# A six-stage transformer kernel: cross attention in pairs of steps on TensorE, two ternary weights quantized in an earlier stage, and another ending

## The chip, the cores and the metric

The kernel runs on one core of a Trainium2 chip. A core has five engines with an instruction queue each: TensorE (PE; its weight loads are listed as PEld), VectorE (DVE), ScalarE (ACT), GpSimd (POOL) and SyncE (SP), which issues most of the DMAs. The metric is the device time of one execution in microseconds (us); the time before is the median of three runs.

## The reference

All of it is float32. `x` is (4, 512, 512); `ctx_2048` is the context. Two layers of three stages each, and a layer norm after each stage:

```python
x = _layernorm(x + _L0_attn_ref(x, q_w, q_b, kv_w, kv_b, o_w))    # A: self-attention with rotary embedding
x = _layernorm(x + _L0_xattn_ref(x, ctx, ctx, gamma))             # B: cross attention over features
x = _layernorm(x + _L0_ffn_ref(x, w_gate, w_up, w_down))          # C: ternary feed-forward
x = _layernorm(x + _L1_attn_ref(x, ...))                          # D
x = _layernorm(x + _L1_xattn_ref(x, ctx, mask))                   # E
x = _layernorm(x + _L1_ffn_ref(x, ...))                           # F: 4-bit feed-forward, RMS norm of its output
```

The stages that the change touches, cut to what matters:

```python
def _L0_xattn_ref(q, k, v, gamma):       # 8 heads of 64 features
    qk = einsum('bhdq,bhdl->bhql', qh, kh) / sqrt(64)
    return gamma * einsum('bhql,bhdl->bhdq', softmax(qk), vh)

def weight_quant(w):                     # _L0_ffn_ref: each of gate, up and down becomes -1, 0 or 1, times a scale
    scale = 1.0 / clip(mean(abs(w)), 1e-5)
    return clip(round(w * scale), -1.0, 1.0) / scale

def _L1_ffn_ref(x, ...):                 # its last lines
    y = einsum('bsi,hi->bsh', h, w_down)
    return y / sqrt(mean(y * y, axis=-1) + 1e-6)
```

The rounding needs the mean of a whole weight first, so each weight is read twice.

## The kernel before

**Order of the work.** The four batches of the six stages make 24 tasks, A0 to F3, in the order of `ORDER`: A0 A1 A2 A3 B0 and so on. Each task is a Python generator that emits instructions and yields. `lanes` (L1234 on) takes a piece from each of at most two live tasks in turn; the next task starts when the newest has said "next" and its own batch has left the stage before. Besides, `BESIDE` names background generators, which are advanced by one piece in each round while given tasks run: "C0" (`l0_ffn_scales`) from A1 to A3, "C" (`l0_ffn_weights`) from B0 to B2. `Pipe.later(n, f)` puts a piece of work off by n ticks of its generator. The recorded program then goes through a scheduler, which keeps data dependences and may pull an instruction forward on its engine; `issue_after(ins)` puts what is emitted behind an instruction of the same engine. Each engine works off its queue in order.

**Memory.** PSUM has eight banks under one tag; `pa` and `pb` take a bank (512 float32 a partition). In SBUF, tiles of 2 KB a partition come from rings: `o` (69), `t` (13), `x` (12) and `w` (4).

**Stage A** (`l0_attn`, L330 on). In each batch TensorE makes q and k in eight tiles (`qk`), ScalarE moves each out with its bias (L340, tile `z`), `turn` does the rotary embedding (DVE L349 times sine, POOL L352 times cosine), `join` adds on POOL (L357), and `split` makes a high part on ScalarE (L143, `qkh`) and a low part on DVE (L146, `qkl`), so that three matmuls (L154 to L156) stand for one in float32. POOL also adds `bvo` to `x` (L408) and makes the low parts of the next batch's input (`xTl`, L146). Then come values `v`, scores `as`, softmax, transposes `ap` and `pv`.

**Stage B** (`l0_xattn`, L457 on). A task has 16 steps: four pairs of heads (n) times four row tiles (i). In one step TensorE makes the scores of two heads with three split products each (L526, six matmuls on 64 rows, tile `bs`). One tick later `soft` takes the maximum on DVE (L474) and the exponential on ScalarE (L476, tile `be`), and `norm` takes the reciprocal on DVE (L480) and multiplies on POOL (L482). Six ticks later `turn` transposes (L248, eight transposes of 128x128, tile `bT`) and copies each result to SBUF (L489, `bpT`; three of four on ScalarE, one on DVE). One more tick later `out` multiplies with the context (L498, 64 columns wide, tile `bo`, accumulated over the four row tiles). After the fourth, `add` (L503) and the layer norm's statistics follow on DVE. In each step one yield ends the piece, and the context of the next batch is loaded beside (`l0_xattn_ctx`, `kf`, `kh`, `kl`).

**Ternary weights.** Gate (`wg_t`), up (`wu_t`) and down (`wd_t`) have 16 chunks of 128x512 each. In A1 to A3, `l0_ffn_scales` loads each chunk into a `w` buffer and sums its absolute values on DVE (L558), and makes mean and scale (L566 to L572). In B0 to B2, `l0_ffn_weights` loads each of the 48 chunks again and quantizes it: two DVE instructions (L587: times the scale plus a large number, which rounds; L588: clip), and a cast to bf16 on ScalarE (L596) into a `tb` tile, two chunks a tile, which stays until stage C's matmuls have read it.

**The end** (`l1_ffn`, b = 3). After the last matmul of F3 (L1168, tile `facc`) ScalarE squares the four results with row sums (L1214), DVE makes the reciprocal root with integer tricks and three Newton steps (`rsqrt`, L166 to L176), adds to `x` (L1220), takes the layer norm's statistics (L211, L212), makes a second root of the same kind and normalizes four tiles (L235); SyncE stores them (L238).

Of the kernel before, what the change touches and what calls it, by code (L numbers as in the profile page):

```python
# [22 lines left out]
P = 128  # L23
NT = 4
# [44 lines left out]
class Net:  # L69
    def __init__(self, ctx, tc, args):  # L70
# [22 lines left out]
        self.gu_codes = scratch("gu_codes", (22, P, 512))  # L93
        self.xd = [args["x"]] + [scratch(f"x{i}", (B, S, D)) for i in range(1, 6)] + [args["out"]]
# [235 lines left out]
    def l0_attn(self, b):  # L330
# [7 lines left out]
        def evac(ps, w, m):  # L338
            z = zs[w, m] = self.t("z")
            nc.scalar.activation(z, ps, AF.Identity, bias=self.qkb[:, w * NT + m : w * NT + m + 1], scale=1.0 if w else P ** -0.5)  # L340
            if m % 2:
                pipe.later(1, turn, w, zs[w, m - 1], z)
# [114 lines left out]
    def l0_xattn(self, b):  # L457
# [26 lines left out]
        def turn(n, es, j, po):  # L484
            pTs = []
            for h in range(2):
                pt = self.transpose4(es[h], j, "bT")
                pT = self.t("bpT")
                (nc.scalar.copy if h == 0 or j % 2 else nc.vector.tensor_copy)(pT, pt)  # L489
                pTs.append(pT)  # L490
            pipe.later(1, out, n, j, po, pTs)

        def out(n, j, po, pTs):
            if j == 0:
                po.append(self.pb("bo"))
            for h in range(2):
                c = n * P + h * 64
                nc.tensor.matmul(po[0][h * 64 : h * 64 + 64, :], cT[j][:, c : c + 64], pTs[h], start=j == 0, stop=j == NT - 1)  # L498
            if j == NT - 1:
                pipe.later(1, add, n, po[0])  # L500
# [8 lines left out]
        yield  # L509
        for n in range(NT):  # L510
            u, es, po = us.pop(n), [[], []], []
            for i in range(NT):
                pipe.tick()
                if (n, i) == (0, 2) and b + 1 < B:
                    self.bg["B", b + 1] = self.l0_xattn_ctx(b + 1)
                if b + 1 < B and ("B", b + 1) in self.bg:
                    next(self.bg["B", b + 1], None)
                if i == 0 and n + 2 < NT:
                    scaled(n + 2)
                sm = self.s("bsm", 6, 8)  # L520
                ps = [self.pa("bs") for h in range(2)]

                for m, (l, r) in enumerate(((0, 0), (1, 0), (0, 1))):
                    for h in range(2):
                        q = slice(h * 64, h * 64 + 64)
                        nc.tensor.matmul(ps[h], u[l][q, i * P : (i + 1) * P], k[n][r][q, :], start=m == 0, stop=m == 2)  # L526
                for h in range(2):
                    pipe.later(1, soft, ps[h], sm, h, i, es)
                pipe.later(1, norm, sm, es, i)
                pipe.later(6, turn, n, es, i, po)  # L530
                yield "next" if 4 * n + i == B_NEXT else None
# [11 lines left out]
    def l0_ffn_scales(self):  # L543

        nc = self.nc
        self.had = self.c("had", [P, P], F32R)
        self.had16 = self.load(self.c("had16", [P, P]), self.a["had16"])
        f = self.t("had")
        nc.gpsimd.dma_start(f[:, 0:P], self.a["had"])
        pipe = Pipe()  # L550
        pipe.later(3, nc.vector.tensor_copy, self.had, f[:, 0:P])
        for name in self.TERNARY:
            chunks = self.ternary_chunks(name)
            part = self.c(name + "_abs", [P, len(chunks)])

            def absum(f, n):
                with self.tc.issue_after(self.mark.ins):
                    nc.vector.tensor_reduce(part[:, n : n + 1], f, AX.X, ALU.add, apply_absolute_value=True)  # L558

            for n, (k, c, ap) in enumerate(chunks):  # L560
                pipe.tick()
                pipe.later(1, absum, self.load(self.w("tw"), ap), n)
                yield
            yield from pipe.drain()
            m = self.c(name + "_mean", [P, 4])
            nc.vector.tensor_reduce(m[:, 2:3], part, AX.X, ALU.add)  # L566
            yield
            ps = self.pb("tot")
            nc.tensor.matmul(ps[:, 0:1], self.ones, m[:, 2:3], start=True, stop=True)
            yield  # L570
            nc.vector.tensor_scalar(m[:, 0:1], ps[:, 0:1], 1.0 / (len(chunks) * P * 512), 1e-5, ALU.mult, ALU.max)
            nc.vector.reciprocal(m[:, 1:2], m[:, 0:1])  # L572
            self.mean[name], self.scale[name] = m[:, 0:1], m[:, 1:2]

    def l0_ffn_weights(self):

        nc = self.nc
        yield from self.bg["C0"]
        pipe = Pipe()
        order = [("wg_t", x) for x in self.ternary_chunks("wg_t")]  # L580
        up = [("wu_t", x) for x in self.ternary_chunks("wu_t")]
        order = [e for c in range(4) for e in order[4 * c : 4 * c + 4] + up[4 * c : 4 * c + 4]]
        order += [("wd_t", x) for x in self.ternary_chunks("wd_t")]
        cur = []

        def quant(name, k, c, f):
            nc.vector.tensor_scalar(f, f, self.scale[name], MAGIC, ALU.mult, ALU.add)  # L587
            nc.vector.tensor_scalar(f, f, MAGIC + 1.0, MAGIC - 1.0, ALU.min, ALU.max)  # L588
            pipe.later(1, put, name, k, c, f)

        def put(name, k, c, f):
            if not cur:
                cur.append(self.o("tb", BF16, 1024))
            o = cur[0][:, 0:512] if len(cur) == 1 else cur[0][:, 512:1024]
            cur.append(o)
            nc.scalar.activation(o, f, AF.Copy, bias=-MAGIC)  # L596
            self.tern[name][k, c] = o
            if len(cur) == 3:
                cur.clear()

        for name, (k, c, ap) in order:
            pipe.tick()
            pipe.later(1, quant, name, k, c, self.load(self.w("tw"), ap))
# [512 lines left out]
    def l1_ffn(self, b):  # L1116
# [31 lines left out]
        def gate(o):  # L1148
            nc.scalar.activation(o, o, AF.Silu)
# [44 lines left out]
        if b + 1 < B:  # L1194
# [16 lines left out]
            return  # L1211
        for i in range(NT):
            sq = self.t("fsq")
            nc.scalar.activation(sq, acc[i], AF.Square, accum_out=ss[:, i : i + 1])  # L1214
            if i % 2:
                yield
        nc.vector.tensor_scalar(ve, ss, 1.0 / 512.0, 1e-6, ALU.mult, ALU.add)
        r = self.rsqrt(ve, fm[:, 8:20])
        for i in range(NT):
            nc.vector.scalar_tensor_tensor(x[i], acc[i], r[:, i : i + 1], x[i], ALU.mult, ALU.add)  # L1220
            self.ln_stats(x[i], i, ln)
            if i % 2:
                yield
        self.finish(pipe, x, ln, 5, b)
        yield from pipe.drain()
# [35 lines left out]
def body(tc, args, phases=range(6)):  # L1261
    with ExitStack() as ctx:
# [4 lines left out]
        net.bg = {("B", 0): net.l0_xattn_ctx(0), "C0": net.l0_ffn_scales(), "C": net.l0_ffn_weights(), "D": net.l1_attn_weights(), "F0": net.l1_ffn_codes(), "F": net.l1_ffn_weights()}  # L1267
# [82 lines left out]
```

## Time and profile before

| what | value |
|---|---|
| median of three runs | 1586.2 us (1585.69 to 1587.84) |
| profiled execution | 1587.75 us |
| its span, first to last instruction | 1586.0 us |
| mean granted clock of TensorE | 0.993 |
| PE busy | 1515.5 us (96%), 8222 matmuls |
| DVE busy | 1239.8 us (78%) |
| ACT busy | 1014.6 us (64%) |
| POOL busy | 666.0 us (42%) |
| DMA | 192.31 MB, mean 121 GB/s |

All durations below come from the profiled execution; its own time is 1.75 us over its span. An instruction's row in a timeline gives its start in us from the span's start, its duration, its engine and line, what it writes and reads, and in brackets the engine's idle time before it and what ended that. A group's row gives the number of instructions, the busy time in us, the mean of one in ns, and the idle time before them. "Slices" are 40 equal parts of the span with the busy share in tenths. A busy TensorE is not TensorE at its peak, since its matmuls overlap and their ends are modelled; the distances between their starts tell more.

### The profile page before, as it was taken

The numbers are of one execution on the slowest core, as the hardware profiler recorded it, in microseconds if no ns is written. First come the engines' busy times: TensorE is split into PE (matmuls) and PEld (weight loads), VectorE is DVE, ScalarE is ACT, GpSimd is POOL, SyncE is SP. The second block draws the span as 40 slices with busy tenths as digits, with TensorE's granted clock in tenths as the row PEclk, the third lists the DMA queues.
The fourth block names the chain that finished last, engine by engine and source line by source line (L and its number), as shares of the span: only waits on it lengthen the run. The fifth ranks groups of instructions, "written<-read, shape, count | busy, mean of one in ns | idle before, by whom it ended". The sixth has DMA issues, their size and how long they took to land.

```text
span 1586.0 us, 25593 instructions
## 1 busy us (share of the span) xinstructions
PE 1515.5 (96%) x8222; PEld 1092.0 (69%) x8222; DVE 1239.8 (78%) x2676; ACT 1014.6 (64%) x2193; POOL 666.0 (42%) x672
## 2 busy tenths in 40 slices
PE   8999999999999999899999999999999999999995
PEld 6888785444544664477777768777687767787874
DVE  6486589999976688778577697766886897889896
ACT  5333337888878877787696765968635455545552
POOL 6663663555535303430435323353234344434341
PEclk9999999999999999999999999999999999999998
DMA  7053344455114644653444435543426630020101
GB/s 254 29 166 114 121 155 136 141 173 184 62 57 123 220 150 131 204 178 116 134 109 122 111 131 153 156 112 91 136 99 219 236 107 30 1 80 1 54 1 53
DMA packets 134149, 192.31 MB, mean 121 GB/s; under 512 B 17264, under 2 KB 52080, under 8 KB 134016
## 3 DMA queue, kind: packets, MB, share of 16 engines
q1 hardware_dynamic: 129888, 182.23, 36.3%
q0 software_dynamic: 4128, 8.46, 2.1%
q8 instruction: 65, 1.06, 0.3%
q14 instruction: 68, 0.56, 0.1%
HBM read 117.75 MB, written 47.71 MB: 104 GB/s over the span
## 4 chain that ended last, share of the span: by engine, by line
PE 61%; DVE 17%; ACT 8%; issue 7%; DMA 3%; POOL 3%; SPq 0%; DVEq 0%; ACTq 0%; POOLq 0%
PE fg L1185 7%; PE facc L1168 6%; PE dT L933 3%; DVE fg L1141 3%; DVE bsm L474 3%; PE pg L687 2%; PE pu L689 2%; PE dn L741 2%; ACT de L923 2%; PE had L755 2%; PE bo L498 2%; PE do L953 2%; PE qk L156 2%; PE qk L155 2%; PE qk L154 2%
## 5 line engine op out<-in xcount | busy, mean ns | idle before, releaser
L1141 DVE SCALAR_TENSOR_TENSOR fg<-fg,gs,fg 128x512 f32<-128x512 f32 x220 | 162.7, 744 | 29.1 <-ACT fg L1133 16.0
L923 ACT ACTIVATE de<-de,dm 128x128 f32<-128x128 f32 (+3 forms) x256 | 143.0, 563 | 11.4 <-DVE dm L919 11.0
L1185 PE MATMUL fg<-fxh,gu 128*128 128x512 f32 x352 | 140.4, 399 | 6.0 <-DVE fg L1141 4.3
L919 DVE CUSTOM_DVE_ANT_0 de<-ds,negm,thr 128x128 f32<-128x128 f32 (+3 forms) x256 | 126.3, 545 | 19.0 <-PE ds L908 15.8
L482 POOL TENSOR_SCALAR be<-be,bsm 128x512 f32<-128x512 f32 x128 | 96.4, 766 | 103.8 <-DVE bsm L480 68.2
L1185 PE MATMUL fg<-fxl,gu 128*128 128x512 f32 x352 | 137.3, 390 | 0.0
L664 POOL TENSOR_TENSOR hl<-g,hh 128x512 fp32r<-128x512 f32 x64 | 83.3, 1308 | 110.6 <-ACT hh L663 89.8
L1145 POOL TENSOR_TENSOR fg<-fg,fg 128x512 f32<-128x512 f32 x44 | 60.4, 1374 | 150.0 <-DVE fg L1141 54.7
L476 ACT ACTIVATE be<-bs,bsm 128x512 f32<-128x512 f32 x128 | 87.4, 690 | 31.1 <-DVE bsm L474 29.3
L845 POOL TENSOR_TENSOR dql<-dqf,dqh 128x512 fp32r<-128x512 f32 x32 | 41.4, 1294 | 150.6 <-ACT dqh L844 141.6
L933 PE MATMUL dT<-ident,de 128*128 128x128 f32 x640 | 91.3, 278 | 8.5 <-ACT de L923 6.4
L933 PEld LDWEIGHTS dT<-ident,de 128*128 128x128 f32 x640 | 71.7, 141 | 27.6 <-ACT de L923 14.8
L1185 PEld LDWEIGHTS fg<-fxh,gu 128*128 128x128 f32 x352 | 66.0, 188 | 31.2 <-DVE fg L1141 15.6
L474 DVE TENSOR_REDUCE bsm<-bs 128x1 f32<-128x512 f32 x128 | 83.3, 671 | 0.0
L498 PE MATMUL bo<-bpT,cT 128*64 128x512 f32 x256 | 77.0, 618 | 2.7 <-DVE bpT L489 1.4
L248 PEld LDWEIGHTS bT<-ident,be 128*128 128x128 f32 x512 | 54.9, 141 | 34.1 <-issue 10.4
L248 PE MATMUL bT<-ident,be 128*128 128x128 f32 x512 | 73.2, 281 | 3.7 <-POOL be L482 2.2
L1185 PEld LDWEIGHTS fg<-fxl,gu 128*128 128x128 f32 x352 | 66.1, 188 | 12.2
L352 POOL TENSOR_TENSOR z<-z,rope_cos 128x512 f32<-128x512 f32 x32 | 46.8, 1473 | 64.8 <-DVE zs L349 57.8
L1137 ACT ACTIVATE fg<-fg,gs 128x512 f32<-128x512 f32 x44 | 30.3, 689 | 67.3 <-PE fg L1185 67.2
L687 PE MATMUL pg<-qT,tb 128*128 128x512 bf16 x256 | 66.8, 381 | 4.5 <-ACT qT L649 2.8
L1133 ACT ACTIVATE fg<-fg,gs 128x512 f32<-128x512 f32 x88 | 60.1, 683 | 16.4 <-PE fg L1185 16.3
(342 smaller groups left out, 4673.2 us busy)
## 6 DMA issues: line engine op xcount, KB each, us to landing
x<-x SPq DMA_DIRECT2D x176, 256.0 KB, 3.0
had_scratch<-hw SPq DMA_DIRECT2D x64, 256.0 KB, 2.3
z<-had_scratch SPq DMA_DIRECT2D x64, 256.0 KB, 6.0
stk<-dqh SPq DMA_DIRECT2D x192, 64.0 KB, 2.1
tw<-in_wg_t SPq DMA_DIRECT2D x32, 256.0 KB, 3.8
tw<-in_wu_t SPq DMA_DIRECT2D x32, 256.0 KB, 3.7
tw<-in_wd_t SPq DMA_DIRECT2D x32, 256.0 KB, 2.8
p<-in_gu_p SPq DMA_DIRECT2D x22, 256.0 KB, 3.1
```

The costliest lines, as they stand in the source:

```text
L248: self.nc.tensor.transpose(pt[:, i * P : (i + 1) * P], srcs[i][:, j * P : (j + 1) * P], self.ident)
L474: nc.vector.tensor_reduce(sm[:, h : h + 1], ps, AX.X, ALU.max, negate=True)
L476: nc.scalar.activation(e, ps, AF.Exp, bias=sm[:, h : h + 1], accum_out=sm[:, 2 + h : 3 + h])
L482: nc.gpsimd.tensor_scalar(es[h][i], es[h][i], sm[:, 4 + h : 5 + h], 1.0, ALU.mult, ALU.mult)
L498: nc.tensor.matmul(po[0][h * 64 : h * 64 + 64, :], cT[j][:, c : c + 64], pTs[h], start=j == 0, stop=j == NT - 1)
L687: nc.tensor.matmul(pg, tern["wg_t"][k, c][:, m], qT[k], start=k == 0, stop=k == NT - 1)
L919: nc.vector.tensor_tensor_reduce(es[i], ps, self.negm[:, 384 - P * i :], -1.0, self.thr[:, i : i + 1], ALU.add, ALU.min, n4[:, i : i + 1])
L923: nc.scalar.activation(es[i], es[i], AF.Exp, bias=n4[:, i : i + 1], scale=-1.0, accum_out=den[:, hh * 4 + i : hh * 4 + i + 1])
L933: nc.tensor.transpose(pt[:, o + (i - j) * P : o + (i - j + 1) * P], es[i][:, j * P : (j + 1) * P], self.ident)
L1141: self.emitted["DVE"] = nc.vector.scalar_tensor_tensor(y[u], ps, s, y[u], ALU.mult, ALU.add)
L1168: nc.tensor.matmul(acc[t], h[l][:, c], self.dn[i][r], start=i == 0 and n == 0, stop=i == 10 and n == 2)
L1185: nc.tensor.matmul(ps, self.gu[i, u][:, g * P : (g + 1) * P], xT[g][n], start=n == 0, stop=n == 1)
```

## The change

1. **Stage B takes two row tiles in one piece.** Scores of tiles i and i+1 are emitted one after the other (twelve matmuls), `turn` transposes for both (sixteen), `out` multiplies for both (four products); `turn` comes three ticks later, a tick being two steps. The generator still yields once a step.
2. **Gate and up become ternary in stage A.** While the absolute sums of the next weight run, the chunks of the one before are loaded into `o` buffers, multiplied and rounded by ScalarE, clipped by POOL, cast by ScalarE, and stored in bf16 to a scratch in HBM (`tern_kept`). In stage B only down is quantized, as before; the 16 tiles of gate and up are loaded back (one down chunk and one kept tile alternate, over 48 yields).
3. **The end** uses Ln and Exp on ScalarE and one Newton step for both roots, with an activation table loaded after the last Silu; the row sums of `x` come with the addition on DVE, the sums of squares from ScalarE, and two of the four normalizations are done by ScalarE.

The diff, cut to its core:

```diff
 # l0_xattn
-        def turn(n, es, j, po):
+        def turn(n, es, js, po):
             pTs = []
-            for h in range(2):
-                pt = self.transpose4(es[h], j, "bT")
-                pT = self.t("bpT")
-                (nc.scalar.copy if h == 0 or j % 2 else nc.vector.tensor_copy)(pT, pt)
-                pTs.append(pT)
-            pipe.later(1, out, n, j, po, pTs)
+            for j in js:
+                for h in range(2):
+                    pt = self.transpose4(es[h], j, "bT")
+                    pT = self.t("bpT")
+                    (nc.scalar.copy if h == 0 or j % 2 else nc.vector.tensor_copy)(pT, pt)
+                    pTs.append((j, h, pT))
+            pipe.later(1, out, n, po, pTs)
...
-            for h in range(2):
+            for j, h, pT in pTs:
                 c = n * P + h * 64
-                nc.tensor.matmul(po[0][h * 64 : h * 64 + 64, :], cT[j][:, c : c + 64], pTs[h], start=j == 0, stop=j == NT - 1)
+                nc.tensor.matmul(po[0][h * 64 : h * 64 + 64, :], cT[j][:, c : c + 64], pT, start=j == 0, stop=j == NT - 1)
...
-            for i in range(NT):
+            for i in range(0, NT, 2):
                 pipe.tick()
...
-                sm = self.s("bsm", 6, 8)
-                ps = [self.pa("bs") for h in range(2)]
...
-                pipe.later(6, turn, n, es, i, po)
-                yield "next" if 4 * n + i == B_NEXT else None
+                for ii in (i, i + 1):
+                    sm = self.s("bsm", 6, 8)
+                    ps = [self.pa("bs") for h in range(2)]
+                    for m, (l, r) in enumerate(((0, 0), (1, 0), (0, 1))):
+                        for h in range(2):
+                            q = slice(h * 64, h * 64 + 64)
+                            nc.tensor.matmul(ps[h], u[l][q, ii * P : (ii + 1) * P], k[n][r][q, :], start=m == 0, stop=m == 2)
+                    for h in range(2):
+                        pipe.later(1, soft, ps[h], sm, h, ii, es)
+                    pipe.later(1, norm, sm, es, ii)
+                pipe.later(3, turn, n, es, (i, i + 1), po)
+                for ii in (i, i + 1):
+                    beside((n, ii) == (0, 2))
+                    yield "next" if 4 * n + ii == B_NEXT else None
 # new
+    def ternary(self, pipe, name, done, early=False):
+        nc = self.nc
+        cur = []
+        def quant(n, f):
+            if early:
+                with self.tc.issue_after(self.turned.ins):
+                    nc.scalar.activation(f, f, AF.Copy, bias=MAGIC, scale=self.scale[name])
+                pipe.later(1, clip, n, f)
+            else:
+                nc.vector.tensor_scalar(f, f, self.scale[name], MAGIC, ALU.mult, ALU.add)
+                nc.vector.tensor_scalar(f, f, MAGIC + 1.0, MAGIC - 1.0, ALU.min, ALU.max)
+                pipe.later(1, put, n, f)
+        def clip(n, f):
+            with self.tc.issue_after(self.joined.ins):
+                nc.gpsimd.tensor_scalar(f, f, MAGIC + 1.0, MAGIC - 1.0, ALU.min, ALU.max)
+            pipe.later(3, put, n, f)
+        def put(n, f):
+            if n % 2 == 0:
+                cur.append(self.o("tb", BF16, 1024))
+            o = cur[0]
+            with self.tc.issue_after(self.turned.ins):
+                nc.scalar.activation(o[:, n % 2 * 512 : n % 2 * 512 + 512], f, AF.Copy, bias=-MAGIC)
+            if n % 2:
+                cur.clear()
+                done(n // 2, o)
+        return quant
 # l0_ffn_scales, now l0_ffn_ternary
+        def keep(name, n, o):
+            pipe.later(1, lambda: nc.sync.dma_start(self.tern_kept[name][n], o.bitcast(F32)))
...
+                pipe.later(1, absum, self.load(self.w("tw"), chunks[n][2]), part, n)
+                if old:
+                    pipe.later(2, quant, n, self.load(self.o("tq"), todo[n][2]))
                 yield
 # l0_ffn_weights
+        for n, (name, m) in enumerate(order):
+            pipe.tick()
+            pipe.later(1, quant, n, self.load(self.w("tw"), self.ternary_chunks("wd_t")[n][2]))
+            yield
+            pipe.tick()
+            o = self.o("tb", BF16, 1024)
+            self.load(o.bitcast(F32), self.tern_kept[name][m])
+            use(name, m, o)
+            yield
             yield
 # l1_ffn, the end of b = 3
+        with self.tc.issue_after(self.silu.ins):
+            table = self.tc.keep_in_program_order(nc.scalar.preload_act_table_set(LOG_EXP))
+        def root(ve, y, t):
+            with self.tc.issue_after(table.ins):
+                nc.scalar.activation(y, ve, AF.Ln)
+            nc.scalar.activation(y, y, AF.Exp, scale=-0.5)
+            self.newton(ve, y, t)
...
         for i in range(NT):
-            nc.vector.scalar_tensor_tensor(x[i], acc[i], r[:, i : i + 1], x[i], ALU.mult, ALU.add)
-            self.ln_stats(x[i], i, ln)
-            if i % 2:
-                yield
-        self.finish(pipe, x, ln, 5, b)
-        yield from pipe.drain()
+            nc.vector.scalar_tensor_tensor(x[i], acc[i], r[:, i : i + 1], x[i], ALU.mult, ALU.add, accum_out=tot[:, i : i + 1])
+            sq = self.t("fsq")
+            nc.scalar.activation(sq, x[i], AF.Square, accum_out=sqs[:, i : i + 1])
+        nc.vector.tensor_scalar(mean, tot, 1.0 / 512.0, None, ALU.mult)
+        nc.vector.tensor_tensor(m2, mean, mean, ALU.mult)
+        nc.vector.tensor_scalar(m2, m2, 1e-5, None, ALU.subtract)
+        nc.vector.scalar_tensor_tensor(v2, sqs, 1.0 / 512.0, m2, ALU.mult, ALU.subtract)
+        root(v2, r2, t2)
+        nc.vector.scalar_tensor_tensor(off, mean, -1.0, r2, ALU.mult, ALU.mult)
+        for i in range(NT):
+            if i % 2:
+                nc.vector.tensor_scalar(x[i], x[i], mean[:, i : i + 1], r2[:, i : i + 1], ALU.subtract, ALU.mult)
+            else:
+                nc.scalar.activation(x[i], x[i], AF.Identity, bias=off[:, i : i + 1], scale=r2[:, i : i + 1])
+            nc.sync.dma_start(self.xd[6][b, i * P : (i + 1) * P, :], x[i])
```

## The prediction

> **What bounds the kernel now.** I read the slices first, then the busy time by stage, then the order of TensorE's instructions inside the stage that the change rewrites. Stages are told apart by their tiles: self-attention A from 6 to 258 us (`qk`, `v`, `as`, `ap`, `pv`), cross attention B from 241.5 to 460.8 (`bs`, `bT`, `bo`), then C (feed-forward) to 760, D and E to 1271, F to 1568.7 and an end to 1586.0. The slices, 39.65 us each:
>
> ```profile
> PE   8999999999999999899999999999999999999995
> DVE  6486589999976688778577697766886897889896
> ACT  5333337888878877787696765968635455545552
> POOL 6663663555535303430435323353234344434341
> ```
>
> PE shows 9 nearly everywhere, but its ends are modelled; the digits that move are DVE's: 9 in the seventh to eleventh slice (238 to 436 us), which are B0 to B2 and a piece of B3. In A it has room, and ScalarE stands at 3. By stretches (A2, A3; B1, B2, B3):
>
> ```profile
> core 0: us, PE busy (x) PEld busy (x) DVE busy (x) ACT busy (x) POOL busy (x), PEclk, DMA share, GB/s
> 110.00:160.00 50.00, 50.00 (x231) 41.36 (x230) 33.51 (x64) 16.91 (x34) 19.21 (x15) 1.00 0.31 100
> 160.00:210.00 50.00, 48.26 (x218) 38.67 (x217) 28.88 (x44) 19.17 (x36) 32.91 (x25) 1.00 0.39 126
> 297.70:351.30 53.60, 51.26 (x289) 25.56 (x288) 51.05 (x113) 46.94 (x116) 29.51 (x37) 1.00 0.51 158
> 351.30:403.90 52.60, 50.45 (x289) 25.44 (x288) 52.06 (x116) 47.59 (x116) 30.35 (x38) 1.00 0.49 158
> 404.00:448.00 44.00, 43.74 (x270) 23.01 (x270) 38.06 (x87) 34.41 (x86) 22.31 (x33) 1.00 0.14 49
> ```
>
> B1 and B2 take 53.6 and 52.6 us for 16 steps each (3.32 us a step) with DVE at 95 and 99%: DVE ends the wait there. In B3, where hardly any ternary work is left, DVE is at 87% and a step takes 2.92 us: there TensorE is the bound. One B3 step on PE:
>
> ```profile
> 433.52 0.50 PE L526 MATMUL bs<-kh,qh 64*128 64x512 f32 x2
> 433.85 0.39 PE L526 MATMUL bs<-kh,ql 64*128 64x512 f32 x2
> 434.08 0.40 PE L526 MATMUL bs<-kl,qh 64*128 64x512 f32 x2
> 434.41 1.09 PE L248 MATMUL bT<-ident,be 128*128 128x128 f32 x8
> 435.43 1.08 PE L498 MATMUL bo<-bpT,cT 128*64 128x512 f32 x4
> 436.44 0.49 PE L526 MATMUL bs<-kh,qh 64*128 64x512 f32 x2
> ```
>
> The reader is to see that the starts are not evenly spaced. Inside `bs` a pair of matmuls follows in 0.23 us, but the first and the last pair take 0.33: 0.20 us a step is spent where the 64-row form begins and ends. The eight transposes start 0.109 us apart (0.873 us), yet 1.02 passes until `bo`: 0.15 more. `bo` takes 1.01 with no run of two steps in this trace to compare.
>
> **Part 1, two steps at a time.** The work is the same (8,222 matmuls); the three forms now alternate once in two steps. Saved in a pair: 0.20 + 0.15, and for `bo` between 0 and 0.15 (the transposes' own value). I take 0.07, midway, since no row shows it: 0.42 a pair, so TensorE's own period falls from 2.923 to 2.71 a step (bounds 2.67 and 2.75). In the changed program PE's order is 12 `bs`, 16 `bT`, 4 `bo` (each two passes), so every copy of a `bT` still has a whole `bs` and `bT` group between it and the `bo` that reads it.
>
> **Part 2, ternary moved.** Out of B go 32 of 48 chunks: on DVE L587 (0.51 to 0.55 us) and L588, on ScalarE L596. The groups of 258 to 461 us (instructions, then busy us, mean ns of one):
>
> ```profile
> L482 POOL TENSOR_SCALAR be<-be,bsm 128x512 f32<-128x512 f32 x120 | 90.6, 768 | 77.8 <-DVE bsm L480 42.2 <-PE bT L248 15.3 <-PE bs L526 10.1
> ...
> L596 ACT ACTIVATE tb<-tw 128x512 bf16<-128x512 f32 x42 | 25.9, 636 | 0.0
> ...
> L588 DVE TENSOR_SCALAR tw<-tw 128x512 f32<-128x512 f32 x44 | 21.9, 508 | 0.2
> ```
>
> DVE loses 32 x 1.04 = 33 us, ScalarE 32 x 0.636 = 20 us. B0 to B2 had 53.8 + 51.1 + 52.1 = 157 us of DVE and 139 of ScalarE in 162.4 us (241.5 to 403.9); that leaves 124 and 119. TensorE needs 48 x 2.71 = 130 us there and 10.9 for A3's 48 `pv` matmuls at 0.227. So TensorE becomes the bound, with DVE and ScalarE at 80 to 85%. Just as B1 and B2 ran a few per cent over DVE's own time, I take 2.80 a step for B0 to B2 (0.09 of waits) and 2.75 for B3: 48 x 2.80 + 10.9 = 145.3, **17.1 us less**; 16 x (2.923 - 2.75), **2.8 less**. With no waits at all and 2.67 it would be 23.3 and 4.0.
>
> What A gets: 32 times an ACT multiply-add (nearest row L630, 0.72), a POOL clip (nearest L482, 0.77), an ACT cast (0.64): 44 us of ScalarE, where it is idle for two thirds, and 25 us of POOL. New waits: the ACT multiply-add waits for its load; behind it on ACT stand the evacuations of `qk` (L340) and the casts `qkh`, `vh`, `aph`, for which PE waits. The clip waits for ACT; behind it on POOL stand the joins (L357) and `xTl`. The store of a ternary tile waits on SP for the cast; behind it stand loads of `tw`, `xT`, `x`. The `xT` loads have 30 us in hand (issued at 140.2, split at 171.3). DMA gains 4.2 MB of stores and 4.2 of loads, net; its share is under 0.53. Where it hurts: A2's last `qkl` ends at 169.0, and `as` starts at 168.6; POOL then runs 165.1 to 176.3 without a gap (four `x`+`bvo`, four `xTl`), and PE waits for `xTl`. In the changed order four clips lie in that stretch before the last `xTl`: 4 x 0.77 = 3.1 us on the path; the other batches have fill on PE (`pv`, `v`) and I give them 1 together: **4 us more**. Bounds: 0, if PE's other lane covers it, and 10, if A3's end loses as much again and the loads come late twice.
>
> [...]
>
> **Part 3, the end.**
>
> ```profile
> 1569.47 0.17 DVE L1217 TENSOR_SCALAR fm<-fm 128x4 f32<-128x4 f32 x1 [7.18 <-ACT fsq L1214]
> ...
> 1571.85 1.41 DVE L1220 SCALAR_TENSOR_TENSOR x<-facc,fm,x 128x512 f32<-128x512 f32 x2
> ...
> 1580.35 1.91 DVE L235 TENSOR_SCALAR x<-x,ln 128x512 f32<-128x512 f32 x4
> 1580.93 1.79 SPq L238 DMA_DIRECT2D out_dram<-x  x4
> ```
>
> Everything from 1569.47 is one chain on DVE. The first root takes 2.38 us; the form with Ln and Exp takes 1.27 where it is free (L220 at 156.95 to the next DVE instruction at 158.22). So the four additions start at 1570.74 and end at 1573.6 (0.70 apart); the squares run beside them on ScalarE, the last ends 0.7 later, 1574.3; second root 1.27 plus the variance's and the offset's 0.2 each end at 1575.8; two normalizations on each engine, 0.65 each on ScalarE, end at 1577.1, against 1582.26. **5.1 us less**; the stores behind stay as long. The activation table's load is 1.28 us in the rows and falls into 3.8 us of ScalarE's idle time before the first square (1566.77); uncovered it would cost that 1.28.
>
> **Sum.** -17.1 - 2.8 + 4 - 5.1 = -21.0 us. The profiled execution took 1587.75 (span 1586.0, 1.75 around it), 1.55 over the median; 1587.75 - 21.0 - 1.55 = 1565.2, so **1565**. PE's order in C to F is unchanged.
>
> **Rivals.** (a) PSUM bounds B, and the kernel is slower. A pair holds four banks of scores and four of transposes beside `bo`'s one: nine, with eight there. For: some transposes in the changed program take over the bank of a group only three groups before them. Against: their copy (0.55) has 1.3 us or a whole `bo`. If each pair waits for an exponential and a copy (0.69 + 0.60), a step takes 2.71 + 0.65 = 3.36: B0 to B2 172.2 (+9.8), B3 +7.0, A +4, end -5.1: +15.7, **1602**. It decides from a wait of some 0.8 us a pair (3.11 a step), where all gains are spent. 10%. (b) A's chain takes every clip: 32 x 0.77 = 25 us in place of 4; **1586**, no change. For: POOL's chain has no slack at A3. Against: its 64 idle us of 131 in 110 to 241. 5%. (c) Runs of two steps save nothing on PE, the gaps being each group's own latency; only DVE's relief counts: 48 x 2.95 + 10.9 = 152.5, -9.9, B3 0: -11, **1575**. 18%. (d) No waits, 2.67, A free: -23.3 - 4.0 - 5.1 = -32.4, **1554**. 12%. My forecast has 55%, with 1559 to 1571 of its own.
>
> **Range and chances.** 1552 to 1580 takes in the forecast, (c) and (d), 85%; (a) and (b) lie outside. Faster by over 0.2% (3.2 us, about what a measurement can tell from no change): 55 + 18 + 12 = 85%, of (b) most is within 0.2%: 6% with the edges; slower 9%.
>
> **What would show it.** Right: `bs` groups of two steps some 5.4 to 5.7 us apart from 245 to 440; first `pg` near 445 (461.2 before, +4 from A, -20); DVE at or under 92% in B1 and B2; last normalization within 8 us of the first root's start. Wrong: PE waiting in front of `bT` or `bs` for ACT copies in every pair (a), `pv` or `as` of A3 more than 5 us late (b), 0.33 and 0.15 still standing in front of every second step (c).

## The result, and the profile after

The changed kernel takes **1611.54 us** (median of four runs, 1610.21 to 1614.58) against 1587.02 (1585.69 to 1591.28) of the kernel before, run beside it: ratio 1.0156, 95% interval 1.0141 to 1.0171. It is slower by 24.5 us, where 21 less were forecast. The profiled execution took 1611.64 us, its span is 1609.9, and the mean granted clock 0.982.

Read along PE's order, the loss has three places. The first `bs` stands at 261.6 us (241.5 before): **A is 20.1 us longer**. From there to the first `pg` it takes 228.2 us (219.7): **B is 8.5 longer**. From the first `pg` to the last `facc` it is 1107.3 (1107.5), nothing. From there to the end of the span 12.9 (17.3): **the end is 4.4 shorter**. Of the page's slices, those that changed:

```profile
PE   8999896888999999899999999999998999999996
DVE  6486576878767578877667788767786898898886
PEclk9999997999999999999999999999999999999998
```

DVE's row of nines from the seventh slice is gone, as intended, but PE's nines there went with it, and the seventh slice of the granted clock reads 7. By stretches (end of A; B1; B3):

```profile
core 0: us, PE busy (x) PEld busy (x) DVE busy (x) ACT busy (x) POOL busy (x), PEclk, DMA share, GB/s
241.00:262.00 21.00, 7.83 (x34) 6.08 (x35) 7.99 (x19) 11.71 (x26) 3.85 (x6) 0.68 0.76 246
...
312.70:368.70 56.00, 49.33 (x292) 28.82 (x290) 43.37 (x90) 42.28 (x106) 29.39 (x36) 0.91 0.40 132
...
422.30:470.00 47.70, 43.33 (x266) 24.86 (x264) 36.79 (x80) 33.03 (x87) 22.65 (x32) 0.96 0.15 51
```

At the end of A no engine is full (ScalarE, the busiest, 11.7 of 21 us) and DMA is at 76%: everything waits for something. In B1 and B3 no engine but PE is near full (DVE 77%), and PE itself stands idle for 6.7 of 56.0 and 4.4 of 47.7 us: it waits for a chain, and its clock falls to 0.91 and 0.96 (1.00 before).

**The end of A.** PE's order of time there, then ScalarE's, then the queue of SP:

```profile
247.55 0.33 PE L249 MATMUL ap<-ident,ae 128*128 128x128 f32 x1 [3.27 <-ACT ae L401]
251.26 0.47 PE L249 MATMUL ap<-ident,ae 128*128 128x128 f32 x1 [3.38 <-ACT ae L401]
...
261.61 0.80 PE L532 MATMUL bs<-kh,qh 64*128 64x512 f32 x2 [5.71 <-ACT qh L470]
```

```profile
236.20 0.72 ACT L561 ACTIVATE tq<-tq,wu_t_mean 128x512 f32<-128x512 f32 x1 [6.74 <-DMA tq<-in_wu_t]
...
237.87 0.67 ACT L401 ACTIVATE ae<-as,asm 128x512 f32<-128x512 f32 x1
...
245.31 0.72 ACT L561 ACTIVATE tq<-tq,wu_t_mean 128x512 f32<-128x512 f32 x1 [6.68 <-DMA tq<-in_wu_t]
```

```profile
225.32 7.39 SPq L253 DMA_DIRECT2D tq<-in_wu_t  x2
```

PE waits for exponentials (`ae`) that have no long wait of their own (1.9 us at most). They stand behind L561 in ScalarE's queue, the quantization of `up`, and that waits for its `tq`: 18.2 us in four waits from 205 to 262. PE's second wait (251.26) comes from there too, by way of DVE: the row maxima for that exponential stand on DVE behind a layer norm, and its root on ScalarE stood behind L561.

```profile
246.87 0.58 DVE L175 TENSOR_TENSOR ln<-ln 128x4 f32<-128x4 f32 x1 [10.71 <-ACT ln L225]
```

The group of two loads at 225.32 shows why. One went out at once, the next at 232.38. Between them SP waited 6.7 us, by the profile for POOL's L409, the last reader of `bvo`, so for a buffer of the ring `o`; what stands behind on SP (`cT`, `tw`, stores, the `x` of B0) waited too. It is not the only such wait: before the group, from 217 to 225, SP stood 5.5 us for a cast on ScalarE whose tile it was to store, and 4.0 for DVE's sums of `down`.

**B.** PE's waits from 262 to 490, the longest by far:

```profile
PE bT L249 <- POOL be L483: 18.2, 15, 3.2
```

In before the same line, in the same window, reads 2.2 us. The distances between pairs of steps (starts of 12 `bs`) are, in B1: 12.8, 3.5, 4.7, 6.4, 11.5, 5.4, 5.9, 5.8. The 5.4 is PE's own period. The 12.8 at the batch's start holds two groups of transposes beside its waits, and the distances behind it are shorter for that; the 11.5 after the fourth pair holds a wait of 3.2. B2 and B3 have the same picture.

**The end** is as forecast:

```profile
1597.81 0.17 DVE L1273 TENSOR_SCALAR fm<-fm 128x4 f32<-128x4 f32 x1 [7.19 <-ACT fsq L1272]
...
1599.08 0.75 DVE L1279 SCALAR_TENSOR_TENSOR x<-facc,fm,x 128x512 f32<-128x512 f32 x1
...
1604.26 1.00 DVE L1290 TENSOR_SCALAR x<-x,ln 128x512 f32<-128x512 f32 x2
```

The first root takes 1.27 us (2.38 before); the normalizations begin 6.45 us after the root's start, where it was 10.88.

### The profile page after: what moved, and what is told of

It is laid out like the page before. It is cut to its first block, busy times and chain, and to the rows that moved or that the text cites. A ratio compares the mean times of both kernels' runs of the same rounds, so it can differ in the third digit from the quotient of the medians.

```text
span 1609.9 us, 25684 instructions
## 1 busy us (share of the span) xinstructions
PE 1511.3 (94%) x8222; PEld 1102.1 (68%) x8222; DVE 1213.5 (75%) x2594; ACT 1040.6 (65%) x2240; POOL 687.3 (43%) x704
## 4 chain that ended last, share of the span: by engine, by line
PE 62%; DVE 13%; ACT 10%; issue 6%; POOL 5%; DMA 4%; SPq 1%; ACTq 0%; DVEq 0%; POOLq 0%
PE fg L1233 7%; PE facc L1216 5%; PE dT L981 3%; PE bT L249 3%; PE bo L500 3%; DVE fg L1189 2%; ACT de L971 2%; PE pu L737 2%; PE pg L735 2%; PE dn L789 2%; PE do L1001 2%; PE bs L532 2%; PE ds L956 2%; PE pv L155 2%; PE pv L157 2%
## 5 line engine op out<-in xcount | busy, mean ns | idle before, releaser
L249 PE MATMUL bT<-ident,be 128*128 128x128 f32 x512 | 75.5, 294 | 19.1 <-POOL be L483 18.2
L249 PEld LDWEIGHTS bT<-ident,be 128*128 128x128 f32 x512 | 59.3, 148 | 40.6 <-POOL be L483 27.0
L1216 PE MATMUL facc<-p4h,fhh 128*128 128x512 f32 x176 | 69.6, 397 | 0.3 <-DVE fg L1189 0.2
L803 PE MATMUL had<-had,z 128*128 128x128 f32 x512 | 66.8, 280 | 2.8 <-DMA z<-had_scratch 2.2
```

What stands on the lines that cost most here:

```text
L249: self.nc.tensor.transpose(pt[:, i * P : (i + 1) * P], srcs[i][:, j * P : (j + 1) * P], self.ident)
L1216: nc.tensor.matmul(acc[t], h[l][:, c], self.dn[i][r], start=i == 0 and n == 0, stop=i == 10 and n == 2)
```

## The experiments

Times in us; each ratio is to the kernel before, run beside it on the same chip. The chips differ from group to group of runs (before took 1585.8 to 1587.8), so runs are best compared by their ratios. "B" is from the first `bs` to the first `pg`.

| run | what it is | median | ratio, 95% interval | first `bs` | B |
|---|---|---|---|---|---|
| before | | 1587.0 | 1 | 241.5 | 219.7 |
| after | all three parts | 1611.5 | 1.0141 to 1.0171 | 261.6 | 228.2 |
| e1_end | end alone | 1583.0 | 0.9961 to 0.9991 | 241.8 | 219.5 |
| e2_pairs | pairs alone | 1611.1 | 1.0129 to 1.0166 | 242.2 | 244.3 |
| e3_ternary | ternary move alone | 1596.9 | 1.0044 to 1.0093 | 263.3 | 207.7 |
| e4_pairs_end | pairs and end | 1607.8 | 1.0114 to 1.0144 | 242.3 | 244.0 |
| e5_pairs_lag4 | e2, transposes 4 pairs behind, not 3 | 1585.8 | 0.9987 to 1.0014 | 242.3 | 218.3 |
| e6_single_lag5 | before, transposes 5 steps behind, not 6 | 1612.0 | 1.0137 to 1.0182 | 241.2 | 242.9 |
| e17_single_lag7 | before, 7 steps behind | 1591.6 | 1.0020 to 1.0039 | 242.2 | 220.1 |
| e8_after_lag4 | after, 4 pairs behind | 1592.2 | 1.0031 to 1.0056 | 260.6 | 210.6 |
| e9_out_first | e2, `bo` ahead of `bT` | 1600.0 | 1.0048 to 1.0095 | 241.6 | 231.1 |
| e7_ternary_lead5 | e3, `tq` loaded 5 steps ahead, not 2 | 1589.5 | 1.0011 to 1.0043 | 253.0 | 209.5 |
| e10_gate_only | e3, gate alone moved | 1586.8 | 0.9981 to 1.0008 | 247.1 | 211.5 |
| e11_all_mended | after, gate alone, `bo` first | 1594.0 | 1.0020 to 1.0042 | 247.3 | 222.4 |
| e12_lead5_out_first | after, 5 ahead, `bo` first | 1598.9 | 1.0056 to 1.0097 | 253.8 | 219.6 |
| e13_pair_turns | before, `bT` and `bo` in pairs, scores single | 1594.0 | 1.0027 to 1.0060 | | |
| e14_pair_turns_end | the same and the end | 1588.9 | 1.0001 to 1.0020 | 241.3 | 226.7 |
| e15_gate_end | e10 and the end | **1581.8** | 0.9946 to 0.9972 | 246.9 | 211.7 |
| e16_gate_pair_turns_end | e14 and gate alone | 1590.0 | 1.0005 to 1.0027 | 244.4 | 217.7 |
| e18_gate_lead5_end | e15, `tq` 5 ahead | 1582.7 | 0.9959 to 0.9983 | 248.8 | 212.3 |

Theory L: A is late because the loads of `tq` are, in ScalarE's order. Theory S: the pairs leave the softmax too little of PE's time before the transposes that need it. Rivals came with the runs.

### The three parts by themselves

The edits are the diff's own parts, applied to the kernel before one at a time (and pairs with end).

> The kernel before with the new end alone. The traces of before and after give from the last matmul of facc to the end of the span 17.3 us before and 12.9 after, so both theories (the late loads in A, the softmax of the pairs in B) expect 4 to 5 us less than before: 1582. If the end costs something elsewhere (the table load inside the last chunk, Silu displaced), it is 1585 or more.

> The kernel before with the pairs of steps in layer 0's cross attention alone; quantization stays where it was (DVE, in B0 to B2). Theory L (the loss is the ternary work in A: loads that come late in ScalarE's order): the pairs alone gain; first pg near 452, total about 1577 (-9), PE waits before bT under 4 us in all of B. Theory S (the loss in B is the pairs' own: the softmax of two steps must be ready within one pair of matmuls, where it was one step within two): PE waits before bT about 15 us in all, first pg 465 to 472, total 1590 to 1597. Under S the waits stand once in four steps, where a new row block n begins its transposes.

> The kernel before with gate and up made ternary in the self-attention alone; single steps in B, old end. Theory L: ScalarE waits some 18 us for loads of tq between 205 and 262, the first bs comes 15 to 20 us late (257 to 262), and B, relieved of DVE work, gives back 5 to 10: total 1594 to 1600. Theory S: A is late by the same, but single steps take no loss in B: total 1586+20-10, the same range; what tells them apart is the time from first bs to first pg: 219.7 in before, 228.2 in after; S says 205 to 215 here, L says 219 or more if the late wd work is what slows B.

> The pairs and the new end, quantization as before. If the parts add, this is the sum of the two runs: about 1573 by theory L, 1586 to 1593 by theory S.

The end gives 4.6 us. The move costs 9.2: A is 21.8 longer, B 12.0 shorter. The pairs by themselves cost **23.4**, all of it in B, as theory S has it and more. Summed, the parts give +28.0, the change +24.5; pairs and end together +20.2 against a sum of 18.8. In e3_ternary ScalarE waits for `tq` much as in the changed kernel:

```profile
ACT tq L554 <- DMA tq<-in_wu_t: 18.9, 4, 8.0
```

### Is it the lag?

```
-                pipe.later(3, turn, n, es, (i, i + 1), po)     # e2_pairs, after
+                pipe.later(4, turn, n, es, (i, i + 1), po)     # e5_pairs_lag4, e8_after_lag4
-                pipe.later(6, turn, n, es, i, po)              # before
+                pipe.later(5, turn, n, es, i, po)              # e6_single_lag5; 7 in e17_single_lag7
```

> The pairs alone, as in e2_pairs (1611), with one number changed: the transposes of a pair are put in line four pairs behind its scores and not three. Theory S (with three, the softmax of the last two steps of a row block has 5.35 us from the end of its scores to the first transpose that needs it, where four reductions, an exponential, a reciprocal and two normalizations in a row take about 4.9; in before two rows had 5.84 us): the waits before bT fall from 22 us to under 4, the pairs after a batch's fourth take 5.4 us and not 9 to 12, first bs to first pg falls from 244.3 to 210 to 218 (DVE, still with all ternary work, bounds B0 to B2), total 1576 to 1585. Rival theory P (the pairs wait because they hold more PSUM and bpT tiles at once): a longer lag holds no fewer, waits and total stay within 5 us of 1611.

> The kernel before, single steps, with its transposes five steps behind the scores and not six: nothing else changes, so PSUM and tiles in use at once do not grow. Theory S: the softmax of a row block's last step now has 2.92 us where two reductions, an exponential, a reciprocal and two normalizations need about 3.5, so PE waits before bT at each of 16 row blocks, 0.5 to 1.5 us each and more where DVE is full: first bs to first pg 230 to 250 (219.7 in before), total 1596 to 1615. Theory P: no change, 1584 to 1589.

> The changed kernel (1611.5) with the transposes four pairs behind. Theory S: B has its pairs at 5.4 us almost throughout; e3_ternary with single steps took 207.7 us from first bs to first pg, 30 pairs at 0.45 less make 194 to 202; first bs stays at 261.6; total 1611.5 less 26 to 34, so 1577 to 1586. Theory P: within 5 us of 1611.

> The kernel before, single steps, with the transposes seven steps behind the scores and not six: the third point of the row of lags (five gave 1612, six is before). Theory S: at six the waits before bT are only 2.2 us in all, so one step more takes away at most that and lengthens each batch's end by one step's transposes without scores beside them: 1584 to 1590, level. If B's pace in before was still set by this lag, 1576 to 1581.

PE's waits in front of `bT` from 262 to 490, in before, in e2_pairs and in e6_single_lag5:

```profile
PE bT L248 <- POOL be L482: 2.2, 6, 0.6
```

```profile
PE bT L248 <- POOL be L482: 21.9, 23, 2.1
```

```profile
PE bT L248 <- POOL be L482: 16.4, 23, 2.8
```

One number, with no pair in sight, makes the kernel before as slow as the pairs do (B 242.9 against 244.3), and one number takes the pairs' loss away (by the ratios 23 us less in e5, and 18 less in e8 with the changed kernel). So the lag is shown to be the cause of the pairs' loss. `turn` for a block of heads needs the softmax of all four row tiles. In single steps the last of them has two steps of PE's work, 5.84 us. In pairs the last two tiles have one pair, 5.35, and need four reductions 0.60 apart, an exponential (0.69), a reciprocal (0.15) and two normalizations (1.36): 4.6 in a row, if no other instruction stands between on DVE. One place of e2_pairs, the transposes of B2's last block of heads beside B3's first scores:

```profile
419.82 0.44 PE L248 MATMUL bT<-ident,be 128*128 128x128 f32 x2
421.32 0.33 PE L248 MATMUL bT<-ident,be 128*128 128x128 f32 x1 [1.06 <-POOL be L482]
423.18 2.85 PE L248 MATMUL bT<-ident,be 128*128 128x128 f32 x13 [1.53 <-POOL be L482]
```

The transposes of the first two row tiles run, and those of the other two wait for their normalizations. On DVE the four reductions of the last two tiles, whose scores ended at 414.5, did not come 0.60 apart:

```profile
414.92 0.67 DVE L474 TENSOR_REDUCE bsm<-bs 128x1 f32<-128x512 f32 x1
...
415.66 0.66 DVE L474 TENSOR_REDUCE bsm<-bs 128x1 f32<-128x512 f32 x1
416.24 1.11 DVE L470 SCALAR_TENSOR_TENSOR ql<-x,qh 128x512 fp32r<-128x512 f32 x1
...
418.47 1.27 DVE L474 TENSOR_REDUCE bsm<-bs 128x1 f32<-128x512 f32 x2
```

Two `ql`, a copy and small work of the layer norm stand between them, so the transpose at 423.18 comes 8.7 us behind the scores and not 5.35. e17_single_lag7 says that before had nothing to win there: one step more leaves B at 220.1 and costs 4.7 in all (1.6 beyond its forecast).

But a longer lag only brings the pairs level with before: e8 misses the slow end of its forecast by 6 us, and e5 lies 0.8 beyond that of its own. Their waits are others now; e5_pairs_lag4, the longest:

```profile
PE bT L248 <- ACT be L476: 5.5, 6, 1.3
PE bs L531 <- ACT be L476: 3.3, 4, 2.1
PE bT L248 <- ACT bpT L490: 2.2, 3, 0.9
```

These are waits for banks: scores read nothing that an exponential writes, and the program puts the waiting transposes into banks that scores held a moment before, which an exponential still reads. That is rival (a) of the prediction, nine banks wanted and eight there, some 15 us with the smaller lines. In e5 they need not be all that holds B, since DVE is busy there for 204 of the 218 us (201 of 220 in before). In e8 DVE has room (180 of 211), and PE is idle for 13.9 us of B, most of it in the same waits, against 1.9 in e3_ternary with single steps; 31 distances of 5.35 in place of 5.85 would save 15. No run takes the banks' limit away.

### Another order instead of another lag

In e9_out_first `turn` first emits the products of the pair before:

```
+        def turn(n, es, js, po):
+            flush()                       # out(...) of the pair before
             pTs = []
...
-            pipe.later(1, out, n, po, pTs)
+            held.append((n, po, pTs))
+            pipe.later(1, flush, pTs)
```

> The pairs alone with the lag of three, as in e2_pairs (1611), with one thing turned round: in each pair the output products (bo) of the pair before go to PE ahead of the pair's transposes (bT), not behind them. No instruction more or less. Theory S: from the end of a pair's scores to the first transpose that needs its softmax there are now 7.2 us of PE's work (8 bo of 1.87 more) and not 5.35; waits before bT fall from 22 us to under 6, first bs to first pg from 244 to 208 to 216, total 1575 to 1583, below e5_pairs_lag4 (1586) if that one lost its gain to PSUM banks held a pair longer. If the lag of PE's order is not what decides, total stays at 1605 to 1611.

By the ratios it gives 12 of the 23 us back, and misses its forecast by 17: waits for POOL before `bT` fall from 21.9 to 6.1 us, and in their place come waits for banks (`bs` behind `be` 3.3, `bT` behind `bpT` 2.6, and smaller). One place in B3 shows how: the layer norm of the batch before holds DVE from 429.9 to 434.8 (1.2 us of its root, 2.7 of normalizations, two reductions between), the next reductions start at 434.8, and the next 12 `bs` take 3.8 us from 433.9, where 1.66 is their own time.

### What holds A

In e7_ternary_lead5 `pipe.later(2, quant, ...)` becomes 5, so each quantization stands five steps behind the load of its `tq`. In e10_gate_only, `if old:` becomes `if old == "wg_t":`, and `up` is quantized by DVE in B0 to B2, ahead of `down`, with gate's kept tiles loaded between its chunks.

> The ternary move alone, as in e3_ternary (1597), with each tq loaded five steps of the planner ahead of its quantization and not two. Theory L (ScalarE, in order, stands at a quantization whose load was issued too late, and the exponentials of A3 behind it): ScalarE's waits for tq from 205 to 262 fall from 18 us to under 6, the first bs comes at 246 to 252 and not at 263.3, total 1580 to 1588. Rival theory R (the loads come late because the buffer they take is freed late, and SP, in order, stands at them): the same loads wait for the same buffers, first bs within 4 us of 263, total 1593 to 1600.

> The ternary move with gate alone moved to A; up is quantized in B0 to B2 by DVE, with down, as before. Single steps, old end. Theory L (the late tq loads of up at the end of A3 hold ScalarE): no tq is loaded after A2, ScalarE waits for none from 205 to 262, first bs at 243 to 246 (263.3 in e3_ternary, 241.5 in before), B takes 211 to 217 (half of the relief), total 1578 to 1584. If A's loss comes from the work itself on ScalarE and GpSimd, half of the 22 us stay: first bs near 252, total 1588 to 1592.

The longer lead brings the first `bs` from 263.3 to 253.0, less than theory L wanted, and ScalarE's waits for `tq` from 18.9 to 10.3. So part of it is rival theory R: some loads stand at a buffer whenever they are asked for. Without `up` no such wait is left between 205 and 262, and the first `bs` is at 247.1 (243 to 246 were forecast, and 1578 to 1584 in all, where 1586.8 came): of A's 21.8 us, 16.2 are `up`'s and 5.6 are gate's, for 3.8 us of `up`'s relief in B. The 2.6 us that A and B have won by the first `pg` (458.6) are not there any more at the last `facc` (1569.8, 1568.7 in before); where they go was not followed.

### Mends together, and what is left of pairing

> The changed kernel with both mends: gate alone moved to A, and bo ahead of bT. If S and L hold and the parts add: first bs 244, B 198 to 208, end 4.5 less: 1560 to 1572, the first of these below before. If the pairs' gain is lost to PSUM banks or to DVE in B0 to B2, B takes 212 to 216 and the total is 1576 to 1582.

> The changed kernel with bo ahead of bT and with the loads of tq five steps ahead, gate and up both moved. By e7_ternary_lead5 the first bs comes at 253; B with all of DVE's relief 192 to 200 if S holds: 1566 to 1576. The comparison with e11 says whether up's relief of B (some 6 us) is worth its price in A (some 9).

> The kernel before with half of the pairing: transposes and output products go two columns at a time as in the change, but the scores stay single steps (PE: bs6 bT16 bs6 bo8). Four row tiles of scores are never due at once: theory S gives the softmax of two rows the same 5.8 us as in before. If what is left of the pairs' loss with a longer lag (e5_pairs_lag4, e11_all_mended) comes from the paired scores, four banks and four exponentials at once, this kernel has no more waits of PE than before in B, and first bs to first pg falls from 219.7 to 213 to 218 (0.15 to 0.3 us a pair saved, DVE bound in B0 to B2): total 1580 to 1586. If it comes from the paired transposes (four banks of bT at once), waits rise and the total is 1592 or more.

> The same with the new end: 4.5 us less than e13_pair_turns, 1576 to 1581 if paired scores are what is left, 1587 or more if not.

> Single steps, gate alone made ternary in A, new end. e10_gate_only was level with before (first pg 2.6 us earlier, given back later), so by that and the end 1580 to 1583, level with e1_end (1583). If gate's early work is worth its 2.6 us, 1579.

> All that is left standing: gate alone in A, scores in single steps, transposes and outputs in pairs, new end. With DVE relieved in B, PE sets the pace and the 0.15 to 0.3 us a pair count in full: B 205 to 209 (211.5 in e10_gate_only), total 1573 to 1579. If PE's own time is not what sets B's pace even then, 1580 to 1583.

> e15_gate_end (1582) with the loads of gate's tq five steps ahead of their use and not two. In e10_gate_only ScalarE still waited 5.6 us for four loads of tq between 160 and 247, and the first bs came 5.6 us later than in before. If late loads are the whole of that price, first bs at 242 to 244 and total 1577 to 1580; if it is the work itself on ScalarE and GpSimd, first bs stays at 247 and the total at 1580 to 1583.

e13 keeps single scores and pairs only the second half:

```
-                pipe.later(6, turn, n, es, i, po)
+                if i % 2 == 0:
+                    pipe.later(6, turn, n, es, (i, i + 1), po)
```

(The table has no stage times for e13; e14 has the same stage B.) Every forecast of a gain from pairing failed. `up` in A with a longer lead (e12) costs more than `up` in B (e11). e11 takes 10.9 us more in B than e10 with single steps; e16 takes 6.0 more than e15. e13 excludes that the paired scores are the whole of it: paired transposes with single scores still lose 7. Why, is **not settled**. In e14 the waits on PE are small (`bo` for a `bpT` of DVE 3.4, `bT` for POOL 2.7). But the same 88 DVE instructions on `tw` take 52.6 us in B and 44.6 in before, and DVE's whole busy time there rises from 201.0 to 206.7, most of the 7.0 that B lost, in a stage that DVE bounds; those that lengthen have a POOL instruction beside them (see the last section). In e16, with 56 of them, this is less than the loss.

e15 beats both kernels: **1581.8**, 0.4% under before, by the end and gate's move. Most of that is the end; e15, e18 and e1 (1583.0) can't be told apart. In e18 the longer lead did not help: the first `bs` comes at 248.8, so late loads are not gate's price in A.

## Why the prediction was wrong, point by point

**What bounds.** Right: DVE bounds B0 to B2; relieved of it, B in single steps (e3) runs at 5.85 us for two steps in 20 of 31 distances and gains 12.0, where rival (c) had 9.9.

**Part 1, PE's period:** right. Undisturbed pairs follow in 5.35 us, 2.68 a step (2.71 taken, 2.67 the bound). **The step that failed** is the next one, "I take 2.80 a step for B0 to B2 (0.09 of waits)". It looked at the cover of each copy of a `bT` and at the work of each engine, and never asked how long the last softmax of a row block has. The change turns six ticks of one step into three of two: the same distance on paper, but the last two tiles come due together, one pair before their transposes. The chain bs, maximum, exponential, normalization, bT could have been added up from rows of before. The pairs' own part of the forecast was some -10 (-19.9 in B, less the -9.9 that rival (c) gives to DVE's relief); measured are +23.4 alone and +20.5 in B beside the ternary move (228.2 against 207.7).

**Part 2, A:** +4 was taken, 0 to 10 the bounds; the run shows 21.8. The step that failed is "the loads come late twice", priced as a part of 10. I put the price on the clips in POOL's order; the rows show ScalarE standing at `tq`. What stood in the working and was not followed through: a ScalarE instruction that waits for a load has everything behind it wait too, the softmax of A3 among it, and that load waits on SP behind other buffers.

**Part 3:** -5.1 forecast, -4.6 measured (interval 1.4 to 6.2 less). Two small slips stand in its working: its own terms put the end of the second root at 1576.0 and not 1575.8, and the next DVE instruction behind 156.95 starts at 158.10, not 158.22. The 1.27 taken for the root was nevertheless what was measured.

**The rivals.** (a) had the right sign, and 1602. Its mechanism is not what the changed kernel shows: PE waits for POOL, not for banks. It is what comes next once the lag is longer. (b)'s sign showed too (`as` of A3 5.1 late, `pv` 21), again by another engine. (c)'s sign did not: the 0.33 and 0.15 us are saved.

**The signs.** Of 31 distances between pairs, 9 are 5.4 to 5.7; the first `pg` is at 489.8 and not near 445; DVE is at 77 and 83% in B1 and B2 (92 or less was right); the last normalization ends 8.1 us after the first root's start (8 was named).

## What to carry to other kernels

When a software pipeline is regrouped from one step to two, count its lags again in microseconds for the last input that becomes ready, not in ticks: add up the chain between the two engines' instructions, and set it against the work that lies between. Where that chain has no slack, coarser groups on the bounding engine can lose more than their shorter period gains: e2_pairs lost 23.4 us, with 5.35 us for two steps in place of 5.84. Background work that waits for a load doesn't belong into the queue of an engine which also carries the foreground's chain, even if that engine is idle for most of the time: ScalarE was busy for 16.9 and 19.2 of 50 us in A2 and A3 of before, and in e3_ternary A took 21.8 us more.

## What the runs showed of the hardware

**Half clock behind stalls.** In before, no part of B runs under full clock. In the changed kernel 28 us of it run at half. Three stretches of it, in order:

```profile
313.50:316.90 3.40, 1.76 (x13) 0.91 (x10) 2.56 (x7) 3.40 (x9) 2.78 (x4) 1.00 0.03 5
316.90:320.30 3.40, 3.40 (x15) 2.58 (x16) 2.77 (x6) 2.56 (x7) 1.20 (x3) 0.50 0.82 263
320.30:323.70 3.40, 3.40 (x26) 2.05 (x22) 2.90 (x7) 2.26 (x6) 1.60 (x3) 1.00 0.56 194
```

PE was busy for 1.76 of 3.40 us, and the next 3.4 us were granted half, with 15 matmuls in place of 26. In the traces of before and after, half clock stands in 13 stretches: nine of 3.41 us, one of 6.83, one of 17.07, and two that run to the trace's end; within a trace they begin at times a multiple of 3.413 us apart. In windows of that length, laid at those times and without the first 6 us, all seven full-clock windows with PE busy for under 0.44 (0.05 to 0.42) had half clock behind them, and of the 21 with 0.45 to 0.64 six had; behind none that was busier did the clock fall. Each of the 11 stretches that ended did so behind a window of 0.91 or more; one of 0.85 had half clock still behind it. What sets the clock is not shown beyond this order. At most half of those 28 us is lost by it, an estimate from the granted 0.50, and part of that would have been waits anyway. In e2_pairs it is 27 us of B, in e6_single_lag5 10, in e5_pairs_lag4 3; the mean granted clocks of these runs are 0.985, 0.989 and 0.992 (0.993 in before).

**The same DVE instructions, longer.** The 88 `tensor_scalar` on `tw` (128x512, float32) take 519 ns in the mean in B of before and 605 in e14. Those with no POOL instruction beside them are alike in both: 449 ns in before (51 of them) and 454 in e14 (33), 489 at most. With one beside them the mean is 615 in before (37) and 696 in e14 (55). So what lengthens lies beside POOL's work, and e14 has more of that. In A of before, the 10 `qkl` with no POOL instruction beside them take 0.67 to 0.69 us, the 22 with one 0.67 to 1.76 (mean 1.03). No run takes POOL's work away, so that it is the reason is not shown.
